# First context and leftover rows loaded behind the third group's queries, odd scores stored when made, value weights loaded later, orders pinned

## The chip, the cores and the metric

The kernel runs on one core of one Trainium2 chip. The metric is the device time of one execution in microseconds (us). Engines: PE (TensorE, with its weight load PEld), DVE (VectorE), ACT (ScalarE), POOL (GpSimd) and SP (SyncE, which here only issues DMAs). All data are fp32.

## The reference

A perceiver block: x (32 batches of 64 queries, 256 wide) gets a cross-attention over a context of 1601 keys of width 192, with 16 heads of 64, then an RWKV time mix and a feed-forward layer, each behind a layer norm and added to x.

```python
def xattn(query, context, w_q, w_kv, w_out, b_out):        # query = layernorm(x), 32 x 64 x 256; context 32 x 1601 x 192
    q = query @ w_q                                        # 16 heads x 64
    k, v = split(context @ w_kv)
    attn = softmax(einsum('bhqd,bhkd->bhqk', q, k) * 64**-0.5)
    return einsum('bhqk,bhkd->bhqd', attn, v) ... @ w_out + b_out
x = x + xattn(layernorm(x), ctx_768, w_q, w_kv, w_out, b_out)
x = x + rwkv(layernorm(x), ...)          # token shift, Wk/Wv/Wr, a scan over 512 steps, Wo
x = x + ffn(layernorm(x), w1, b1, w2, b2)
```

The change touches only the start of the cross-attention.

## The kernel before, in words

**Folding.** Keys and values are never made. The queries are multiplied by each head's key weights, so that a score is the product of a raw context row (192 wide) and a folded query (192 wide). The attention then averages raw context rows, and the value weights come after that.

**Query stage** (`queries`, L268, up to about 137 us). Four groups tg of 8 batches (512 tokens), each in two halves e of 8 heads. A half has 8 projections q_ps (L292), copied by ACT to a slot of `room[1]` (L299); the folds ql onto context columns 0 to 127 (L313), copied by DVE (L320) and ACT (L321) into q_lo, of which there are two buffers; the folds qh onto columns 128 to 191 (L341), copied by DVE (L348, L352; by ACT at L350 in the last half) into q_hi. Folded queries go to DRAM: two q_lo stores of 1 MB (L323) and two q_hi stores of 512 KB (L355) a half. The context has 1601 = 12 x 128 + 64 + 1 keys; the scores of the last, odd key are made apart (`odd_scores`, L242: matmuls L250, copies L257 and L258 into a buffer `od`) and stored by `odd_store` (four DMAs of 32 KB, L264). `turned_x` (L203) transposes the next group's normalised x; `normed_x` (L189) makes that on DVE. Where the order in the code leaves an engine free, the scheduler of the language places instructions by its own plan, unless `tc.issue_after(x)` pins an instruction behind x.

**Memory shared by stages.** Two large tiles, `room[0]` and `room[1]` (L381), hold weights and projected queries in the query stage. They have the tag of the two score buffers s_sb, so room[0] becomes s_sb of u = 0 and room[1] that of u = 1. `od` has the tag cT (L392), and so shares its two buffers with the transposed keys.

**Attention loop** (L972). u = 0 to 63 are halves of batches: b = u // 2, heads 8 j to 8 j + 7 with j = u % 2. `scores` (L649) makes six tiles of two key chunks, s_ps (L658, two PSUM buffers), each copied by ACT into s_sb (L665), with running maxima on DVE (L667 to L677). Behind the first tile of a batch the leftover 64 keys are scored (rest_ps, L635), from the rows of cT that a DMA copies (L374). `max_all` (L682) takes the maximum over partitions; `exps` subtracts it (DVE L703) and exponentiates (ACT L704), in three pieces, for u = 0 hung on tiles 3 to 5 of u = 1. The half before then gets its weighted sums: o_lo over context columns 0 to 127 (`av_lo`, L468 and, for leftover rows, L809, L819) and o_hi over the rest (`av_hi`, L864), with c_b, the raw context (`ctx_load`, L141), and rows_b, its 64 leftover rows (`rows_load`, L148). `total` (L763) and `inverse` (L776) make the denominators and `keep` (L792) stores them through ACT's queue.

**The order on SP.** Almost every DMA is issued by SP, in program order, each taking one of eight semaphores in turn, so that a ninth waits for the first. After the last query store (L355) SP issues rows_0 (L152), rest (L624), cb_1 (12 pieces of batch 1's keys in blocks, L170), q_1 (L180), c_0 (L143), the eight odd stores of the last group (`odd_late`, L413, run at L1051 to L1053 with `late_loads`), the value and output weights wv_lo, wv_hi, wo (L438 to L441), the RWKV weights (L448), biases and columns (L450 to L458), and then cT_1's row copy (L374).

Of the kernel before, what the change touches and what calls it, by code (L numbers as in the profile page):

```python
# [9 lines left out]
F32 = mybir.dt.float32  # L10
# [5 lines left out]
P = 128  # L16
# [4 lines left out]
def kernel(  # L21
# [38 lines left out]
    nc = tc.nc  # L60
# [6 lines left out]
    C2 = C - P  # L67
    NT = B * T // P
    NP = H // 2
# [5 lines left out]
    NS = C // C2  # L75
# [3 lines left out]
    KT = NBL * BL  # L79
    HALF = H // 2 * T  # L80
# [45 lines left out]
    with ExitStack() as st_b:  # L126
        with ExitStack() as st_a:
# [28 lines left out]
            def blocks_load(b):  # L156
# [16 lines left out]
                            )  # L173
                return c

            def q_load(b):

                q = kp.tile([P, NS, H * T], F32, tag="q", name=f"q_{b}")
                for r0 in (0, C2):
                    nc.sync.dma_start(  # L180
                        q[r0 : r0 + C2, :, :],
                        q_dram[b // QB][b % QB].rearrange("(s p) n -> p s n", p=C2),
                    )
                return q

# [82 lines left out]
            def queries(tg, xnT, copied, sp, sps, wq_sb, wkT, room, codn, kodT, wk_lo, wk_hi, od):  # L268
# [7 lines left out]
                for e in range(NP // 4):  # L276
# [5 lines left out]
                    for g in (2 * e, 2 * e + 1):  # L282
                        slot = (tg * NP // 2 + g) % 5
                        qT = room[1][:, slot * 2 * TG : (slot + 1) * 2 * TG].rearrange(
                            "p (k t) -> p k t", k=2
                        )
                        qTs.append(qT)
                        for k in range(2):
                            hp = 2 * g + k
                            pq = sps.tile([P, TG], F32, tag="ps", name=f"q_ps_{tg}_{hp}")  # L290
                            for c in range(2):
                                projected = nc.tensor.matmul(  # L292
                                    pq,
                                    lhsT=wq_sb[:, c, hp * P : (hp + 1) * P],
                                    rhs=xnT[:, c, :],
                                    start=(c == 0),
                                    stop=(c == 1),
                                )
                            nc.scalar.activation(qT[:, k, :], pq, AF.Copy, scale=HD**-0.5)  # L299
                    if e == 0 and tg == 0:  # L300
                        with tc.issue_after(projected.ins):
# [24 lines left out]
                        )  # L326
                    all_q.append(qTs)
                    for n in (0, 1) if e == 1 and tg == 0 else (e,) if tg else ():
                        odd_scores(tg, n, kodT, all_q[n], od[n], sps)
                        if more:  # L330
                            odd_store(tg, n, od[n])
                        else:
                            odd_late.append(lambda n=n: odd_store(tg, n, od[n]))
                    for k in range(2):
                        ph = [
                            sps.tile([P, QB, T], F32, tag="f", name=f"qh_ps_{tg}_{e}_{k}_{o}", bufs=6)
                            for o in range(2)
                        ]
                        for n in range(2):
                            for o in range(2):  # L340
                                nc.tensor.matmul(  # L341
                                    ph[o][n * C2 : (n + 1) * C2, :, :],
                                    lhsT=wkT[o * HD : (o + 1) * HD, 4 * e + 2 * n + k, P:C],
                                    rhs=qTs[n][o * HD : (o + 1) * HD, k, :],
                                    start=True,
                                    stop=True,
                                )
                        nc.vector.tensor_copy(hi[:, :, 2 * k, :], ph[0])  # L348
                        if e == 1 and not more:
                            nc.scalar.copy(hi[:, :, 2 * k + 1, :], ph[1])  # L350
                        else:
                            nc.vector.tensor_copy(hi[:, :, 2 * k + 1, :], ph[1])  # L352
                    for n in range(2):
                        ns = slice((8 * e + 4 * n) * T, (8 * e + 4 * n + 4) * T)
                        store = nc.sync.dma_start(  # L355
                            q_dram[tg][:, P:C, ns].rearrange("b p n -> p b n"),
                            hi[n * C2 : (n + 1) * C2].rearrange("p b h t -> p b (h t)"),
                        )
# [18 lines left out]
            with tc.tile_pool(name="setup", bufs=1) as sp, tc.tile_pool(  # L377
# [11 lines left out]
                ]  # L389
                wk_hi, codn = wk_hi[0:C2], codn[0:B]  # L390
                kodT = kodT.rearrange("p (h b) -> p h b", b=B)
                od = kp.tile([P, NS * KT], F32, tag="cT", name="od")  # L392
                od = [
                    od[:, k * 2 * TG : (k + 1) * 2 * TG].rearrange("p (o t) -> p o t", o=2)
                    for k in range(2)
                ]
                wq_sb = wq_sb.rearrange("p (c n) -> p c n", c=2)
                wkT = wkT.rearrange("p (h c) -> p h c", c=C)
                wqr = w_q.rearrange("(c p) n -> p c n", p=P)
# [10 lines left out]
                for n in range(4, NT, 4):  # L410
                    nc.sync.dma_start(x_sb[:, n : n + 4, :], xr[:, n : n + 4, :])
                b_tiles = {0: blocks_load(0)}
                odd_late = []  # L413
                for g in range(NP // 2):
                    ps = sps.tile([P, 2, C], F32, tag="ps", name=f"wkT_ps_{g}")
                    for k in range(2):
# [8 lines left out]
                for tg in range(B // QB):  # L425
                    turned, store = queries(tg, *turned, sp, sps, wq_sb, wkT, room, codn, kodT, wk_lo, wk_hi, od)
                    if tg == 1:
                        q_tiles = {0: q_load(0)}
                        cT = ctx_prep(0)

            nats = {}
            aw = st_a.enter_context(tc.tile_pool(name="late", bufs=1))
# [1 line left out]
            wv_hi = aw.tile([P, INNER], F32, name="wv_hi")  # L434
            wo_sb = aw.tile([P, INNER // P, D], F32, name="wo_sb")

            def late_loads():
                nc.sync.dma_start(wv_lo, w_kv[0:P, INNER : 2 * INNER])  # L438
                for r0 in (0, C2):
                    nc.sync.dma_start(wv_hi[r0 : r0 + C2, :], w_kv[P:C, INNER : 2 * INNER])  # L440
                nc.sync.dma_start(wo_sb, w_out.rearrange("(c p) n -> p c n", p=P))  # L441
                tags = iter(("xn", "in_k", "in_v", "in_r", "e", "ev", "num", "den"))
                for n, w in (("Wk", Wk), ("Wv", Wv), ("Wr", Wr), ("Wo", Wo)):
                    nats[n] = [
                        rp.tile([P, D], F32, tag=next(tags), name=f"nat_{n}_{c}") for c in range(2)
                    ]
                    for c in range(2):
                        nc.sync.dma_start(nats[n][c], w[c * P : (c + 1) * P, :])  # L448
                for n, v in enumerate((b_out, bo, b2)):
                    nc.sync.dma_start(bias_rows[:, n, :], v.partition_broadcast(P))  # L450
                with nc.allow_non_contiguous_dma(reason="per-channel vectors"):
                    for n, v in enumerate((time_decay, time_first)):
                        nc.sync.dma_start(cols[:, n, :], v.rearrange("(c p) -> p c", p=P))
                    for n, v in enumerate((mix_k, mix_v, mix_r)):
                        nc.sync.dma_start(
                            cols[:, 2 + n, :], v.rearrange("a b (c p) -> p (a b c)", p=P)
                        )
                    nc.sync.dma_start(b1_sb, b1.rearrange("(c p) -> p c", p=P))  # L458
# [223 lines left out]
            def max_all(u, mx):  # L682
                mb = ap.tile([P, HALF], F32, tag="mb", name=f"mb_{u}")
                nc.gpsimd.partition_all_reduce(mb, mx, P, bass_isa.ReduceOp.max)  # L684
                return mb
# [277 lines left out]
                        x_sb[:, i, :], x_sb[:, i, :], bias_rows[:, 0, :], ALU.add  # L963
                    )

            c_tiles = {}
            rests = [None, None]
            last = None
            before = None
# [2 lines left out]
            for u in range(2 * B):  # L972
# [2 lines left out]
                phase, i = (u - 5) % 4, (u - 5) // 4  # L975
                if before is not None:
                    before.out()
                if j == 0:
                    rows_load(b)
                out, mixer, older = outs[max(i, 0)], mixers[max(i, 0)], mixers[max(i - 1, 0)]  # L980
                fill = {}
# [18 lines left out]
                if u == 1:  # L1000

                    hooks = {3: parts[0:2], 4: parts[2:3], 5: parts[3:]}
                elif last is not None:
                    hooks = {
                        3: [last.inverse] + ([out.share] if phase == 1 and i >= 0 else []),
                        5: [last.keep],
                    }
                    last.total()
                else:
                    hooks = {}  # L1010
                s_sb, mx, top, done = scores(u, cT, q_tiles[b], hooks)
                if j == 0 and b + 1 < B:
                    with tc.issue_after(store.ins):
                        b_tiles[b + 1] = blocks_load(b + 1)
                        q_tiles[b + 1] = q_load(b + 1)
                mb = max_all(u, mx)
                if u == 1:
                    with tc.issue_after(top.ins):
# [8 lines left out]
                if u == 1:  # L1027
                    last.total()
                    last.inverse()
                    last.keep()  # L1030
                if j == 0 and 0 < b < B - 1:
                    cT_next = ctx_prep(b + 1)
                elif j == 1:
                    cT = cT_next
                if phase == 0 and i > 0:
# [6 lines left out]
                    mixer.norm()  # L1042
                if u == 2 * B - 2:
                    ready = stats_of(rp, list(range(4)), "ln3_0", "3")
                if j == 0:
                    c_tiles[b] = ctx_load(b)
                if phase == 3 and i >= -1:
                    odd_load(i + 1)
# [153 lines left out]
```

## Time and profile before

| | |
|---|---|
| time, median of 3 runs | 2555.59 us (2555.51 to 2556.14) |
| profiled execution | 2556.28 us, span 2554.5 us |
| PE busy | 2534.3 us (99%), 15618 instructions |
| DVE busy | 1925.0 us (75%) |
| ACT busy | 985.2 us (39%) |
| POOL busy | 411.2 us (16%) |
| first scores matmul of the attention loop | 137.14 us |
| first o_lo matmul of u = 0 with c_0 | 176.21 us |
| granted TensorE clock, mean | 0.999 |
| DMA | 174.23 MB, mean 68 GB/s |

Times in the profile are counted from the start of the span. A timeline row has start, us, engine, line, operation, out<-in, shapes and count, and in brackets the idle time of the engine ahead of it and what ended that. SPq is SP's sequencer, and its rows are the issuing of DMAs, not the transfers. A row of a table of waits names the instruction that waited and what released it.

### The profile page before, as it was taken

Reading aid. Unit: us, or ns where it says so; the run is one execution under the profiler, and the core shown is the slowest. Engines: PE = TensorE matmul, PEld = TensorE weight load, DVE = VectorE, ACT = ScalarE, POOL = GpSimd, SP = SyncE. Lnnn points to the kernel's source line nnn. Section 1 sums busy time; section 2 is a strip of 40 time slices with the busy share of each in tenths; the row PEclk is TensorE's granted clock in tenths of the full one; section 3 lists DMA queues with packets and bytes.
Section 4 is the critical chain, followed back from the end, with each engine's and each line's share of the span. In section 5 each row is a group of like instructions: output and inputs, shape, how many; then the busy total and the mean of one; then the engine's idle time right before and its main releaser. Section 6 shows DMA issues by size and latency. Waiting matters only on the chain.

```text
span 2554.5 us, 38114 instructions
## 1 busy us (share of the span) xinstructions
PE 2534.3 (99%) x15618; PEld 1215.2 (48%) x15618; DVE 1925.0 (75%) x2364; ACT 985.2 (39%) x1103; POOL 411.2 (16%) x372
## 2 busy tenths in 40 slices
PE   9989999999999999999999999999999999999999
PEld 3334444444444454444444454444444444444466
DVE  5477878878787878878787878878787878777731
ACT  3343434434333444333433344343433334344221
POOL 1002111121111121111111111111111111111100
PEclk9999999999999999999999999999999999999999
DMA  7786333333233223233332323233332322310100
GB/s 202 219 212 112 60 64 62 51 66 65 61 62 61 55 47 66 47 66 66 66 65 55 60 41 66 53 61 66 65 66 53 69 47 51 66 28 20 53 13 21
DMA packets 435967, 174.23 MB, mean 68 GB/s; under 512 B 334960, under 2 KB 421520, under 8 KB 435792
## 3 DMA queue, kind: packets, MB, share of 16 engines
q1 hardware_dynamic: 435408, 171.53, 32.7%
q8 instruction: 122, 2.00, 0.3%
q14 instruction: 53, 0.43, 0.1%
q10 hardware_dynamic: 384, 0.26, 0.0%
HBM read 141.07 MB, written 29.10 MB: 67 GB/s over the span
## 4 chain that ended last, share of the span: by engine, by line
PE 90%; DVE 4%; issue 2%; DMA 1%; SPq 1%; POOL 1%; ACT 1%; DVEq 0%; ACTq 0%; POOLq 0%
PE s_ps L658 35%; PE o_lo L468 24%; PE o_hi L864 11%; PE y_ps L468 2%; PE q_ps L292 2%; PE h_ps L1111 2%; PE fy L1127 2%; PE rest_ps L635 1%; PE o_hi L819 1%; PE v_ps L919 1%; PE ql_ps L313 1%; DVE s_sb L703 1%; PE o_lo L809 1%; DVE m L669 1%; PE v_ps L933 1%
## 5 line engine op out<-in xcount | busy, mean ns | idle before, releaser
L658 PE MATMUL s_ps<-q,cT 64*128 64x512 f32 x4608 | 1008.0, 590 | 2.3 <-ACT s_sb L665 1.4
L658 PEld LDWEIGHTS s_ps<-q,cT 64*128 64x128 f32 x4608 | 443.5, 187 | 516.5 <-issue 497.7
L468 PE MATMUL o_lo<-s_sb,c 128*64 128x512 f32 x3024 | 679.1, 596 | 5.8 <-DMA c<-in_ctx_dram 5.8
L665 ACT COPY s_sb<-s_ps 128x1024 f32<-128x1024 f32 x384 | 388.3, 1011 | 740.3 <-PE s_ps L658 732.2
L703 DVE TENSOR_TENSOR s_sb<-s_sb,mb 128x2048 f32<-128x2048 f32 x192 | 431.5, 2283 | 0.0
L704 ACT ACTIVATE s_sb<-s_sb 128x2048 f32<-128x2048 f32 x192 | 367.1, 1913 | 123.9 <-DVE s_sb L703 123.9
L468 PEld LDWEIGHTS o_lo<-s_sb,c 128*64 128x64 f32 x3024 | 209.3, 137 | 387.6 <-issue 383.3
L669 DVE TENSOR_TENSOR m<-m,s_sb 128x1024 f32<-128x1024 f32 x256 | 312.3, 1220 | 40.7 <-ACT s_sb L665 18.5
L864 PE MATMUL o_hi<-s_sb,c 128*64 128x256 f32 x3024 | 337.0, 379 | 0.0
L769 DVE TENSOR_TENSOR t<-t,s_sb 128x1024 f32<-128x1024 f32 x256 | 311.8, 1218 | 8.6 <-DVE t L769 0.5
L864 PEld LDWEIGHTS o_hi<-s_sb,c 128*64 128x64 f32 x3024 | 217.4, 137 | 135.9 <-issue 36.0
L772 POOL PARTITION_ALL_REDUCE den<-t x64 | 207.1, 3236 | 407.2 <-issue 381.6
L784 DVE STREAM_TRANSPOSE turned<-den 128x512 f32<-128x512 f32 x64 | 45.5, 711 | 275.6 <-POOL den L772 275.6
L693 ACT ACTIVATE rest<-rest 128x512 f32<-128x512 f32 x64 | 40.4, 631 | 405.5 <-DVE rest L692 363.5
L684 POOL PARTITION_ALL_REDUCE mb<-m x64 | 114.2, 1785 | 431.1 <-DVE m L677 417.3
L692 DVE TENSOR_TENSOR rest<-rest,mb 128x512 f32<-128x512 f32 x64 | 44.3, 692 | 108.0 <-POOL mb L684 107.9
L623 POOL MEMSET rest<- 64x256 f32 x128 | 39.2, 307 | 413.6 <-PE o_lo L809 307.7
L372 DVE STREAM_TRANSPOSE cT<-cb 128x768 f32<-128x768 f32 x96 | 89.5, 957 | 0.0
L667 DVE TENSOR_TENSOR m<-s_sb 128x1024 f32<-128x1024 f32 x64 | 77.6, 1212 | 9.1 <-ACT s_sb L665 9.1
L111 POOL TENSOR_TENSOR rstd_ln<-rstd_ln,root 128x1 f32<-128x1 f32 (+1 forms) x24 | 33.7, 1402 | 311.9 <-DVE rstd_ln L110 311.9
L809 PE MATMUL o_lo<-rest,rows 64*128 64x256 f32 x252 | 81.1, 402 | 0.0
L819 PE MATMUL o_hi<-rest,rows 64*128 64x256 f32 x252 | 81.1, 402 | 0.0
(164 smaller groups left out, 1829.3 us busy)
## 6 DMA issues: line engine op xcount, KB each, us to landing
q<-q_dram SPq DMA_DIRECT2D x64, 768.0 KB
c<-in_ctx_dram SPq DMA_DIRECT2D x32, 1152.0 KB
cb<-in_ctx_dram SPq DMA_DIRECT2D x192, 104.0 KB
cb<-in_ctx_dram SPq DMA_DIRECT2D x192, 96.0 KB
q_dram<-q_lo SPq DMA_DIRECT2D x16, 1024.0 KB
q_dram<-q_hi SPq DMA_DIRECT2D x16, 512.0 KB
rows<-in_ctx_dram SPq DMA_DIRECT2D x64, 32.0 KB
rest<-o_dram SPq DMA_DIRECT2D x128, 1.0 KB
```

Of the source, the lines that this page charges most:

```text
L468: last = nc.tensor.matmul(out[rs], lhsT=lhsT[:, rs], rhs=rhs, start=start, stop=stop, skip_group_check=True,)
L658: done = nc.tensor.matmul(ps[:, k, :], lhsT=cT[rs, s, i * P : (i + 1) * P], rhs=q[rs, s, js : js + HALF], start=(s == 0), stop=(s == NS - 1),)
L665: copied = nc.scalar.copy(s_sb[:, 2 * i : 2 * i + 2, :], ps)
L669: nc.vector.tensor_tensor(m2, m2, s_sb[:, 2 * i : 2 * i + 2, :], ALU.max)
L684: nc.gpsimd.partition_all_reduce(mb, mx, P, bass_isa.ReduceOp.max)
L703: nc.vector.tensor_tensor(s, s, m, ALU.subtract)
L704: nc.scalar.activation(s, s, AF.Exp)
L769: nc.vector.tensor_tensor(t2, t2, p[:, 2 * i : 2 * i + 2, :], ALU.add)
L772: nc.gpsimd.partition_all_reduce(self.den, t2[:, 0, :], P, bass_isa.ReduceOp.add)
L809: nc.tensor.matmul(self.po[:, k * HH : (k + 1) * HH], lhsT=self.rows[lo, 0, :], rhs=self.rest[lo, k * HH : (k + 1) * HH], start=(k == 0), ...
L819: nc.tensor.matmul(self.ph, lhsT=self.rows.rearrange("p n c -> p (n c)")[hi, c0 : c0 + P], rhs=self.rest[hi, (1 - k) * HH : (2 - k) * HH], ...
L864: nc.tensor.matmul(self.ph[o * C2 : (o + 1) * C2, :], lhsT=self.ctx[:, self.at[c], P:C], rhs=self.s_sb[:, c, o * HH : (o + 1) * HH], start ...
```

## The change

1. c_0 and rows_0 are loaded right behind the last store of the third group (tg = 2), ahead of the fourth group's stores; the loop no longer loads them for b = 0.
2. `od` leaves the tag cT. od[0] is now the tile m2 (tag m2, later the running maximum), and for the last group a slot of room[1]; od[1] is the part of room[1] behind the five query slots. In the last group the odd scores of n = 0 are stored when made; those of n = 1 stay where the late stores were.
3. wv_lo, wv_hi and wo are loaded in u = 2, behind the last of q_2's loads, and no longer in u = 0.
4. The projections q_ps of a half are pinned behind the last fold of the half before.
5. cT_0's preparation is pinned behind the last q_hi copy of group 1, cT_2's behind the last maximum of u = 2, and `keep` of u = 0 moves from u = 1 to the hook behind tile 2 of u = 2.

```diff
@@ q_load
-                    nc.sync.dma_start(
-                        q[r0 : r0 + C2, :, :],
-                        q_dram[b // QB][b % QB].rearrange("(s p) n -> p s n", p=C2),
+                    fetched.append(
+                        nc.sync.dma_start(
+                            q[r0 : r0 + C2, :, :],
+                            q_dram[b // QB][b % QB].rearrange("(s p) n -> p s n", p=C2),
+                        )
                     )
@@ queries
-                            for c in range(2):
-                                projected = nc.tensor.matmul(
+                            with tc.issue_after(folds[-1].ins) if folds else ExitStack():
+                                for c in range(2):
+                                    projected = nc.tensor.matmul(
...
                     for n in (0, 1) if e == 1 and tg == 0 else (e,) if tg else ():
+                        if not more and n == 0:
+
+                            at = (tg * NP // 2 - 1) % 5 * 2 * TG
+                            od[0] = room[1][:, at : at + 2 * TG].rearrange("p (o t) -> p o t", o=2)
                         odd_scores(tg, n, kodT, all_q[n], od[n], sps)
-                        if more:
+                        if more or n == 0:
                             odd_store(tg, n, od[n])
                         else:
                             odd_late.append(lambda n=n: odd_store(tg, n, od[n]))
...
-                                nc.tensor.matmul(
+                                fold = nc.tensor.matmul(
...
-                        nc.vector.tensor_copy(hi[:, :, 2 * k, :], ph[0])
+                        filed.append(nc.vector.tensor_copy(hi[:, :, 2 * k, :], ph[0]))
...
+                    folds.append(fold)
@@ setup
-                od = kp.tile([P, NS * KT], F32, tag="cT", name="od")
-                od = [
-                    od[:, k * 2 * TG : (k + 1) * 2 * TG].rearrange("p (o t) -> p o t", o=2)
-                    for k in range(2)
-                ]
+                m2 = ap.tile([P, 2, HALF], F32, tag="m2", name="od")
+                od = [m2, room[1][:, 10 * TG : 12 * TG].rearrange("p (o t) -> p o t", o=2)]
...
                     if tg == 1:
                         q_tiles = {0: q_load(0)}
-                        cT = ctx_prep(0)
+                        with tc.issue_after(filed[-1].ins):
+                            cT = ctx_prep(0)
+                    if tg == 2:
+                        with tc.issue_after(store.ins):
+                            rows_load(0)
+                            c_tiles = {0: ctx_load(0)}
@@ late loads
-            def late_loads():
+            def value_loads():
                 nc.sync.dma_start(wv_lo, w_kv[0:P, INNER : 2 * INNER])
...
                 nc.sync.dma_start(wo_sb, w_out.rearrange("(c p) n -> p c n", p=P))
+
+            def late_loads():
@@ attention loop
-                if j == 0:
+                if j == 0 and b:
                     rows_load(b)
...
+                    if u == 2:
+                        hooks[2] = [before.keep]
                     last.total()
...
                         q_tiles[b + 1] = q_load(b + 1)
+                        if u == 2:
+                            with tc.issue_after(fetched[-1].ins):
+                                value_loads()
...
                 if u == 1:
                     last.total()
                     last.inverse()
-                    last.keep()
                 if j == 0 and 0 < b < B - 1:
-                    cT_next = ctx_prep(b + 1)
+                    with tc.issue_after(top.ins) if b == 1 else ExitStack():
+                        cT_next = ctx_prep(b + 1)
...
-                if j == 0:
+                if j == 0 and b:
                     c_tiles[b] = ctx_load(b)
```

More of the change, by code (lines that the diff above doesn't have):

```diff
@@ L174, in blocks_load @@
                 return c
+            fetched = []
             def q_load(b):
@@ L290, in queries @@
                             pq = sps.tile([P, TG], F32, tag="ps", name=f"q_ps_{tg}_{hp}")
-                            for c in range(2):
-                                projected = nc.tensor.matmul(
[L293 to L298, printed above, removed]
+                            with tc.issue_after(folds[-1].ins) if folds else ExitStack():
+                                for c in range(2):
+                                    projected = nc.tensor.matmul(
+                                        pq,
+                                        lhsT=wq_sb[:, c, hp * P : (hp + 1) * P],
+                                        rhs=xnT[:, c, :],
+                                        start=(c == 0),
+                                        stop=(c == 1),
+                                    )
                             nc.scalar.activation(qT[:, k, :], pq, AF.Copy, scale=HD**-0.5)
@@ L412 @@
                 b_tiles = {0: blocks_load(0)}
-                odd_late = []
+                odd_late, filed, folds = [], [], []
                 for g in range(NP // 2):
@@ L964, in yproj @@
                     )
-            c_tiles = {}
             rests = [None, None]
```

## The prediction

> **What bounds the kernel now.** I read the page first: PE is busy 2534.3 of 2554.5 us, so some 20 us in the whole span are not matmul. The change touches the first 220 us only, and what it can win or lose there is the idle time of PE. The table of PE's waits (line, what it waited for, then us in total, times, longest) names that time:
>
> ```profile
> PE o_lo L468 <- DMA c<-in_ctx_dram: 5.8, 1, 5.8
> PE s_ps L658 <- ACT s_sb L665: 1.4, 4, 0.5
> PE ql_ps L313 <- ACT q_lo L321: 1.2, 1, 1.2
> PE rest_ps L635 <- DMA cT<-cT: 1.1, 1, 1.1
> PE ql_ps L313 <- DVE q_lo L320: 1.0, 1, 1.0
> PE s_ps L658 <- ACT q_hi L350: 0.8, 1, 0.8
> ```
>
> The largest is the first value product (o_lo) waiting for batch 0's context c_0. PE's timeline shows where the waits lie, and what follows them:
>
> ```profile
> 137.14 2.85 PE L658 MATMUL s_ps<-q,cT 64*128 64x512 f32 x12 [0.83 <-ACT q_hi L350]
> ...
> 176.21 12.52 PE L468 MATMUL o_lo<-s_sb,c 128*64 128x512 f32 x48 [5.81 <-DMA c<-in_ctx_dram]
> ...
> 194.37 2.74 PE L658 MATMUL s_ps<-q,cT 64*128 64x512 f32 x12
> 198.20 1.53 PE L635 MATMUL rest_ps<-q,cT 64*64 64x256 f32 x24 [1.08 <-DMA cT<-cT]
> 200.05 13.14 PE L658 MATMUL s_ps<-q,cT 64*128 64x512 f32 x60 [0.32 <-ACT s_sb L665]
> ```
>
> The 48 o_lo matmuls take 12.52 us here; in the next batches the chain of waits has them at 10.45. So the wait costs 5.81 + 2.07 us. The granted clock is 0.50 in 176 to 180 us and 0.99 after it. From the first scores tile to the second, it is 200.05 - 194.37 = 5.68 us at the third half against 141.38 - 137.14 = 4.24 at the first: 1.44 us for the waits on cT and s_sb.
>
> Why c_0 is late stands in SyncE's queue (issue time, us spent issuing, line) and in the stretches (us, then busy time of PE, PEld, DVE, ACT, POOL, granted clock, DMA share, GB/s):
>
> ```profile
> 132.56 4.59 SPq L323 DMA_DIRECT2D q_dram<-q_lo  x2
> 137.25 4.96 SPq L355 DMA_DIRECT2D q_dram<-q_hi  x2
> 142.31 7.16 SPq L152 DMA_DIRECT2D rows<-in_ctx_dram  x4
> 149.56 2.62 SPq L624 DMA_DIRECT2D rest<-o_dram  x4
> 152.24 8.43 SPq L170 DMA_DIRECT2D cb<-in_ctx_dram  x12
> 160.72 1.48 SPq L180 DMA_DIRECT2D q<-q_dram  x2
> 162.24 0.60 SPq L143 DMA_DIRECT2D c<-in_ctx_dram  x1
> 162.88 14.16 SPq L264 DMA_DIRECT2D o_dram<-od  x8
> ```
> ```profile
> 148.00:152.00 4.00, 4.00 (x22) 1.85 (x20) 2.34 (x2) 1.02 (x2) 0.00 (x0) 1.00 0.25 68
> 152.00:163.00 11.00, 11.00 (x54) 4.90 (x52) 7.29 (x7) 4.75 (x5) 1.80 (x1) 1.00 0.93 113
> 163.00:171.00 8.00, 7.40 (x38) 3.23 (x34) 7.79 (x6) 6.44 (x7) 0.20 (x1) 1.00 0.98 209
> ```
>
> Transfers run in the order of issue: the last query stores end at about 149 (a share of 0.25 in the 4 us from 148 is 1 us of work), then cb_1 (1.2 MB) to 162, q_1 (1.5 MB) to 170, c_0 behind them, landed at 176.1, and the eight odd stores after it.
>
> **Part by part.** S0 is the first scores matmul, 137.14.
>
> *1. c_0 and rows_0 issued before the last group's stores.* c_0 then lands before S0, and nothing else holds o_lo: its scores' last exponential ends at 173.63, but chunks are taken in an order that needs the first third (168.2) and second (170.9) first. **-5.81**, and **-2.07** for the clock. The price is 1.25 MB, some 5 us at the 252 GB/s of 171 to 176, put in front of the last six MB of stores.
>
> *2. Odd scores out of the key tile cT.* In the timeline cT_1 is transposed only at 178.52, after the odd stores (DMA 176.74 + 1.74 in the chain). Freed of them and of the weight loads on SyncE (177.15 to 194.57, ahead of cT_1's own DMA at 195.04), the rest keys land before they are needed. The odd store n = 0 of the last group is now issued when made; four such issues took 3.54 us of SyncE at 115.79, here between the two halves' stores, where SyncE has nothing else to issue: nothing. With keep of the first half moved behind the third score tile, ScalarE no longer stands in front of the copy that began at 198.98. **-1.44**.
>
> *3. The new wait.* One of the two odd buffers now lies in room[1], the memory that becomes s_sb_1. The late odd store (n = 1 of the last group, four DMAs) is still issued behind cb_1 and q_1. So ScalarE's first copy of the second half (157.14 before) waits until those stores have landed. Queued behind it on ScalarE are the other copies and the exponentials of half 0, hooked to copies 3 to 5; PE has two PSUM buffers, so it goes on for two tiles and stands at the third, which began at 157.14 + 2.36 = 159.50. When do they land? Call D the end of the query stores. From D to the end of q_1 it was 149 to 170 = 21 us, 3 of them idle (148 to 152) while rows and rest waited for free DMA slots; the rows are gone, so 18, and 1.5 to 2 to land (od: 1.74 after c_0's landing): D + 19 to 20, at most D + 23 if the idle time stays.
> D: before, the stores ran from 111.98 to 149, at shares of 0.84, 0.80, 0.78, 0.95, 1.00 and 0.96 in six stretches of 6 us: 4 us idle. After, group 2's last stores are issued about 7 us earlier (21 q_ps records, 9.3 us, ran ahead of its last ql; they are pinned behind it now; less the 2.8 of part 4, so 6.5). 149 - 6.5 + 5 - (0 to 4) is 143.5 to 147.5. It can't be before the last store is made and moved: S0' + 0.1, and 1 MB at 0.2 to 0.3 MB per us, 143.5 to 145. Both ends for D: 143.5, and 149 if nothing is won by the earlier start; I take 146, in the middle of them. Then the stores land at 165.0, the copy ends at 166.1, and PE, due at S0' + 22.4 = 162.3, stands **+3.8** us. From both sides: 1.3 to 10.8 (149 + 23 + 1.1 - 162.3).
>
> *4. q_ps pinned behind the previous half's folds.* The matmuls themselves stay; what goes is their use as filler. In half 1 of group 0, ten q_ps stood between 40.42 and 44.91 while VectorE normalised the next group; the first q_lo copy ends at 42.81 + 0.69:
>
> ```profile
> 42.81 1.88 DVE L320 COPY q_lo<-ql_ps 128x512 f32<-128x512 f32 x3
> ```
>
> so PE now stands from 40.42 to 43.5: +3.1. In group 1 the two q_ps at 70.94 (1.06 us of the way to the copies that end at 74.1) become waiting: +1.06. In the last group, where q_ps records ran between ql and its copies, each half is now whole, and the 1.22 on ACT q_lo goes, with a gap of 0.16 at 134.24: net **+2.8**. Bounds: +0.5 (the group 0 wait met by other work ready at 40.42, such as the transposes of the next group) and +4.2 (3.1 + 1.06 and nothing won). Thus S0' = 139.9.
>
> *5. Clock after the new stall.* At the measured 2.07 per 5.81 us of stall, 3.8 gives **+1.4** (0 to 2.1). The Trainium skill ("TensorE: Matmul & The Clock Gate", Part 1, What's actually happening) says that the gate falls to half after about one idle window of 3.4 us and rises again after one busy window; the 0.50 in 176 to 180 agrees. By it a stall under 3.4 us need cost nothing more and a longer one about 1.7 (an estimate from that page), so the sum would be 0.3 higher, and 1.1 lower for a stall of 3 us.
>
> *6. Weight loads later, orders pinned.* wv and wo are used first at 257.38 (the odd values), some 45 us after q_2's issue at 210.13; 2 MB need 8 us at 252 GB/s: hidden. cT_2 and keep in new places: at most one preparation (2.69 + 0.38 us on DVE) ends in front of PE, and at least nothing; I take **+1.0**.
>
> Sum: +2.8 + 3.8 + 1.4 + 1.0 - 5.81 - 2.07 - 1.44 = -0.3 on the profiled execution's 2556.28 us (span 2554.5 and 1.8 around it): 2556.0. The median of the runs is 2555.59, 0.7 lower; I forecast **2555.7**, nearly what the sum gives on the median, rounded up. The wait for c_0 is swapped for a wait for the odd stores, which stand behind the same two transfers.
>
> The Trainium skill ("DMA: Bandwidth & Descriptors", Queues, rings and completion order) has a rule that speaks against part 3: completion is not first in, first out per issuing engine, so a small store could overtake q_1 on engines that are done early. The trace shows c_0's landing at 176.1 and the first odd landing at 178.5, though issued 0.6 us apart. If the rule carried, the stores would land up to a microsecond or two sooner and the sum would be lower by that.
>
> **The rivals.**
> *A, the gain is realised.* The stores land while PE still has tiles to do or just after: D at its floor of 143.5, landing at 162.5, stall 0 to 1.3, no clock loss, nothing in front of PE in part 6, and a query stage between its lower bound and my value: +0.5 to 2.8, +0 to 1.3, -9.3: -8.8 to -5.2, central 2549. For it: shares of 0.78 to 0.84 before 130 show room to take in c_0 early. Against it: cb_1 and q_1 alone need 16 us at 113 and 209 GB/s, and PE is due 19 us after D's floor.
> *B, slower: the moved 1.25 MB pushes the whole queue.* From 130 to 148 the share is 0.95 to 1.00, so what goes in front there comes out at the end. D = 150.5 to 154, stores landing 170 to 174, or q_lo buffers (two) come free late and PE stands in the query stage instead; either way PE's third tile of half 1 starts at 171 to 175 instead of 159.5: +11.5 to 15.5 (the query stage's 2.8 is in it), +2.1 clock, +1.0, -9.3: +5.3 to +9.3, central 2563. It decides where D passes 149, that is, where the earlier start is worth less than the moved bytes.
> *C, c_0 still late*, so that the change doesn't do its first step: it would need c_0 to land past 170, 50 us after its issue; nothing in the queue is that long. I give it nothing.
>
> **How the numbers follow.** Forecast (stall swapped, own range 2551 to 2560.5): 0.50. A: 0.20. B: 0.30. A measurement tells about 0.2%, 5.1 us, from no change. A lies below 2550.5, B above 2560.7; so faster 0.20, same 0.50, slower 0.30. The range takes in A's centre and B's: 2548 to 2565.
>
> **What would show it.** Right: no wait on DMA c; a new row of s_ps waiting for ACT s_sb of 3 to 7 us at the second half's third tile, ScalarE's copy released by o_dram<-od; a q_lo wait on DVE near 43 of 3 us; S0' near 140; o_lo of half 0 at 10.45. Wrong: S0' over 142 (the stores hold the query stage), a copy released before 160 (A), or a stall over 9 us (B). An added wait at PE after 220 us that is not there before would mean that part 6 was priced too low.

## The result and the profile after

The changed kernel takes 2560.24 us (median of 22 runs, 2556.75 to 2563.45) against 2556.0 us for the kernel before (22 runs, 2555.31 to 2559.83): a ratio of 1.0015, 95% interval 1.0009 to 1.002. It is slower by 4.2 us, inside the 0.2% of no change, and inside the range; the upper end of the forecast's own range, 2560.5, is 0.3 us away. The forecast of 2555.7 missed by 4.5 us. Its terms can be checked one by one, because the profiled span grew by nearly as much as the median, by 4.0 us, from 2554.5 to 2558.5.

PE's waits in the changed kernel (line, what it waited for, us in total, times, longest):

```profile
PE s_ps L672 <- ACT s_sb L679: 8.2, 3, 7.3
PE wkT_ps L425 <- DMA room<-in_L_xattn_w_kv_dram: 4.4, 2, 4.1
PE ql_ps L318 <- DVE q_lo L325: 2.9, 1, 2.9
PE wkT_ps L426 <- DMA room<-in_L_xattn_w_kv_dram: 1.3, 2, 0.9
PE rw_ps_Wr L496 <- ACT Wk_T L501: 1.1, 1, 1.1
```

The wait for c_0 has gone, and so have those on cT and on ACT q_lo. In their place stand 7.3 us for ScalarE's copy of a score tile, 2.9 for q_lo in group 0 and 1.1 for the RWKV weights (`wkT_ps` waits for the first loads in both kernels). PE's timeline shows where:

```profile
44.06 1.97 PE L318 MATMUL ql_ps<-room,room 64*128 64x512 f32 x2 [2.92 <-DVE q_lo L325]
45.96 3.66 PE L254 MATMUL odd_ps<-room,room 64*32 64x512 f32 x32
49.55 2.65 PE L350 MATMUL qh_ps<-room,room 64*64 64x512 f32 x16
...
139.86 2.85 PE L672 MATMUL s_ps<-q,cT 64*128 64x512 f32 x12 [0.84 <-ACT q_hi L359]
...
169.70 12.64 PE L672 MATMUL s_ps<-q,cT 64*128 64x512 f32 x48 [7.31 <-ACT s_sb L679]
...
182.70 10.52 PE L482 MATMUL o_lo<-s_sb,c 128*64 128x512 f32 x48
```

The third tile of the second half starts at 169.70; o_lo of half 0 runs without a wait in 10.52. The chain of waits says what the third tile waited for (start, us, what):

```profile
141.16 9.21 DMA q_dram<-q_hi
150.39 0.52 SPq L170
...
156.56 7.41 DMA q<-q_dram
164.03 4.57 DMA nat_Wv<-in_L_attn_Wv_dram
168.63 1.02 ACT s_sb L679
169.70 12.64 PE s_ps L672 x48
```

In order stand the last query store, cb_1 (L170), q_1, then the copy. The chain names a load of an RWKV weight as the last releaser. The copy doesn't read it: SyncE's queue (issue time, us spent issuing, line) has the four late odd stores at 158.14, between q_1 and the RWKV weights, and the profile infers releasers from semaphores that the DMAs take in turn. By the semaphore events in the trace the four odd stores landed at 167.69 to 168.49, just ahead of the copy at 168.63, and the first load of nat_Wv only at 169.93:

```profile
116.95 5.50 SPq L152 DMA_DIRECT2D rows<-in_ctx_dram  x4
122.50 0.59 SPq L143 DMA_DIRECT2D c<-in_ctx_dram  x1
...
156.56 1.53 SPq L183 DMA_DIRECT2D q<-q_dram  x2
158.14 1.57 SPq L268 DMA_DIRECT2D o_dram<-room  x4
159.75 0.85 SPq L462 DMA_DIRECT2D nat_Wk<-in_L_attn_Wk_dram  x2
```

c_0 is issued 40 us earlier than before. Experiment e1 takes the odd stores away from there.

Laid beside each other, in us (the predicted column is the running sum of the prediction's terms):

| mark | before | after | difference | predicted |
|---|---|---|---|---|
| first scores matmul | 137.14 | 139.86 | +2.7 | +2.8 |
| third tile of half 1 | 159.50 | 169.70 | +10.2 | +6.6 |
| o_lo of half 0 | 176.21 | 182.70 | +6.5 | +2.2 |
| first tile of u = 2 | 194.37 | 198.87 | +4.5 | +0.1 |
| second tile of u = 2 | 200.05 | 202.99 | +2.9 | -1.3 |
| first tile of u = 3 | 232.67 | 236.75 | +4.1 | -0.3 |
| span | 2554.5 | 2558.5 | +4.0 | -0.3 |

Nearly the whole error, 3.6 of 4.3 us, is there at the second mark, the third tile of half 1.

### The profile page after: what moved, and what is told of

Read it like the earlier page. It is cut to its first block, busy times and chain, and to the rows that moved or that the text cites. A ratio compares the mean times of both kernels' runs of the same rounds, so it can differ in the third digit from the quotient of the medians.

```text
span 2558.5 us, 38118 instructions
## 1 busy us (share of the span) xinstructions
PE 2535.4 (99%) x15618; PEld 1214.2 (47%) x15618; DVE 1927.7 (75%) x2364; ACT 986.0 (39%) x1103; POOL 412.8 (16%) x372
## 4 chain that ended last, share of the span: by engine, by line
PE 93%; DVE 4%; DMA 1%; issue 1%; POOL 1%; ACT 0%; SPq 0%; DVEq 0%; ACTq 0%; POOLq 0%
PE s_ps L672 36%; PE o_lo L482 24%; PE o_hi L878 12%; PE y_ps L482 2%; PE q_ps L297 2%; PE h_ps L1129 2%; PE fy L1145 2%; PE rest_ps L649 2%; PE o_hi L833 1%; PE v_ps L933 1%; PE ql_ps L318 1%; DVE s_sb L717 1%; PE o_lo L823 1%; PE v_ps L947 1%; PE qh_ps L350 1%
## 5 line engine op out<-in xcount | busy, mean ns | idle before, releaser
L683 DVE TENSOR_TENSOR m<-m,s_sb 128x1024 f32<-128x1024 f32 x256 | 316.1, 1235 | 42.9 <-ACT s_sb L679 20.5
```

Of the source, the lines that this page charges most:

```text
L683: nc.vector.tensor_tensor(m2, m2, s_sb[:, 2 * i : 2 * i + 2, :], ALU.max)
```

## The experiments

Theory S is the prediction's: the new stall is the late odd store, which stands behind cb_1 and q_1. Rival Q is that the moved 1.25 MB push the whole queue; rival P that the pinned projections are the loss. Each run stood beside runs of the kernel before on the same chip (medians 2555.9 to 2556.5).

| run | what | us | ratio to before, 95% interval |
|---|---|---|---|
| e1 | after, all odd scores stored when made | 2552.29 | 0.9981 (0.9972 to 0.999) |
| e2 | after, no pins of q_ps | 2564.87 | 1.0035 (1.0021 to 1.0048) |
| e3 | before, c_0 and rows_0 early alone | 2564.32 | 1.0032 (1.002 to 1.0045) |
| e4 | before, new place of the odd scores alone | 2581.07 | 1.0098 (1.0084 to 1.0112) |
| e5 | e1, pins in groups 2 and 3 only | 2552.06 | 0.9984 (0.9975 to 0.9993) |
| e6 | e1, keep in its old place | 2558.79 | 1.001 (1.0001 to 1.0018) |
| e7 | e1, c_0 and rows_0 in their old place | 2560.77 | 1.0014 (1.0005 to 1.0023) |
| e8 | before, pins alone | 2559.82 | 1.0015 (1.0006 to 1.0024) |
| e9 | e1, pins in group 3 only | 2549.13 | 0.9971 (0.9959 to 0.9982) |
| e10 | e9, keep of u = 1 later | 2548.48 | 0.9969 (0.9957 to 0.9981) |
| e11 | e7, PE's order as in e1 | 2551.79 | 0.9982 (0.9973 to 0.9991) |
| e12 | e1, value weights in their old place | 2554.75 | 0.9991 (0.9982 to 1.0) |

**e1: the late odd store stored when made.**

```diff
-                        if more or n == 0:
-                            odd_store(tg, n, od[n])
-                        else:
-                            odd_late.append(lambda n=n: odd_store(tg, n, od[n]))
+                        odd_store(tg, n, od[n])
```

> The changed kernel, but the last group's odd scores of n = 1 are stored when made as well, ahead of the last q_hi stores, so that no store stands behind cb_1 and q_1. Theory S (the stall at the second half's third score tile is the wait for that late store, behind cb_1 and q_1): the first copy of the second half runs at 160, the 7.31 us stall and its slow clock (12.64 against 10.4 for 48 matmuls, 2.2) go: 2560.2 - 7.3 - 2.2 = 2550.7. Rival Q (the 1.25 MB moved ahead push the whole queue, so that something behind the query stores is late whatever is first): a wait of 4 to 7 us comes back at PE between 160 and 205, on cT, q or rest: 2556 to 2560. Rival P (the pinned q_ps are the loss): 2560 less the stall only as far as they allow, and first scores matmul still at 139.9; with S it is also there, so P is read from the next run.

2552.29, which is 8.0 less than the changed kernel. PE's timeline in u = 0 to 2:

```profile
142.23 28.59 PE L669 MATMUL s_ps<-q,cT 64*128 64x512 f32 x132
...
171.19 10.52 PE L479 MATMUL o_lo<-s_sb,c 128*64 128x512 f32 x48
...
193.37 13.14 PE L669 MATMUL s_ps<-q,cT 64*128 64x512 f32 x60 [1.81 <-ACT s_sb L676]
```

The eleven score tiles run in one piece, without the stall and at full clock. That shows the stall to be the wait for the late store. One small wait comes up later, 1.81 at u = 2's second tile: ScalarE's queue there has the exponentials of half 1, and these wait for DVE. Q's 4 to 7 us don't appear.

**e2: without the pins of q_ps.** `with tc.issue_after(folds[-1].ins) if folds else ExitStack():` becomes `with ExitStack():`.

> The changed kernel without the pins of q_ps behind the previous half's folds. Theory S: the first scores matmul comes back to about 137.1, but the third group's last stores are issued some 6 us later again, with the moved 1.25 MB behind them, so the query stores end at 149 to 154, the late odd store lands 19.3 later, and the second half's third tile starts at 170 to 174 (169.7 with pins): 2560 to 2565, nothing won. Rival P (the 2.7 us that the query stage is longer is the loss): 2557.4.

2564.87, 4.6 more than with pins; rival P falls. But the form was not the expected one: the first scores matmul came at 144.22, not at 137.1, because of a wait in the query stage, and the stall at the third tile was 6.44.

```profile
136.82 2.20 PE L318 MATMUL ql_ps<-room,room 64*128 64x512 f32 x4 [4.72 <-ACT q_lo L326]
...
144.22 2.85 PE L672 MATMUL s_ps<-q,cT 64*128 64x512 f32 x12 [0.85 <-ACT q_hi L359]
...
173.19 12.05 PE L672 MATMUL s_ps<-q,cT 64*128 64x512 f32 x48 [6.44 <-ACT s_sb L679]
```

```profile
136.21 1.29 DVE L325 COPY q_lo<-ql_ps 128x512 f32<-128x512 f32 x2 [5.29 <-DMA q_dram<-q_lo]
```

DVE's own wait at that place, 5.29 us, is on a q_lo store: both q_lo buffers stood behind c_0 in the queue. So the early load needs the pins, which bring group 2's last stores forward (107.86 against 111.81 here).

**e3: the early load alone.**

```diff
+                    if tg == 2:
+                        with tc.issue_after(store.ins):
+                            rows_load(0)
+                            c_tiles = {0: ctx_load(0)}
...
-                if j == 0:
+                if j == 0 and b:
                     rows_load(b)
...
-                if j == 0:
+                if j == 0 and b:
                     c_tiles[b] = ctx_load(b)
```

> The kernel before, with c_0 and rows_0 loaded behind the third group's last store and nothing else changed. Theory S: the wait for c_0 (5.81) and its slow clock (2.07) go, the wait on cT (1.4) stays, and the odd scores stay in the memory of cT, where nobody on PE waits for them before 178: 2556.0 - 7.9 = 2548.1. Rival Q: the moved bytes delay the last group's stores, PE stands for q_lo buffers or cT_1 waits longer for the odd stores (which land at 170 to 174 and hold DVE's transposes): 2552 to 2556.

2564.32: neither number. The waits are Q's, but they cost 8 to 12 us more than Q's 2552 to 2556. In the list of PE's waits:

```profile
PE ql_ps L313 <- ACT q_lo L321: 5.5, 2, 4.2
PE s_ps L662 <- ACT s_sb L669: 5.0, 3, 4.7
...
PE rest_ps L639 <- DMA cT<-cT: 3.4, 1, 3.4
```

The wait for c_0 has gone, yet nothing is won. 4.2 us go to the q_lo buffers, as in e2. And at u = 2 the waits on cT (1.1 before, 3.4 now) and on s_sb (4.7, ScalarE itself standing 8.10 us for the denominators rden) take what the c_0 wait had covered.

**e4: the new place of the odd scores alone**, which adds their wait to the old order.

> The kernel before, with the new place of the odd scores alone: m2 and room[1], n = 0 of the last group stored when made, n = 1 late, behind cb_1, q_1 and here c_0 too. Theory S: the first copy of the second half waits until that store lands at about 177, the third tile starts at about 178.5 instead of 159.5 (+19), the wait for c_0 disappears inside it (-7.9) and the cT wait (-1.4), the clock loss comes back (+2.2): 2556 + 12 = 2568. Against it (the copy waits for something else than the store): 2554 to 2556.

2581.07. ScalarE's copy and PE's third tile:

```profile
177.75 1.93 ACT L666 COPY s_sb<-s_ps 128x1024 f32<-128x1024 f32 x2 [21.96 <-DMA o_dram<-room]
...
194.03 1.01 ACT L666 COPY s_sb<-s_ps 128x1024 f32<-128x1024 f32 x1 [4.61 <-DMA b_sb<-in_L_ffn_b_dram]
```
```profile
178.81 12.37 PE L659 MATMUL s_ps<-q,cT 64*128 64x512 f32 x48 [18.93 <-ACT s_sb L666]
...
222.72 15.17 PE L659 MATMUL s_ps<-q,cT 64*128 64x512 f32 x60 [8.89 <-ACT s_sb L666]
```

Here the profile names the odd store as the releaser. The stall was expected at 19 and is 18.93. Of the 13 us above the forecast, 10.6 stand at PE in two waits that I had not priced: 1.71 on the exponentials, behind 4.61 at ScalarE, whose own two stores of the leftover exponentials take their semaphores in turn with SyncE's small loads and came behind them (they were issued at 192.70 and 193.79, when the loads that had held these two semaphores landed, at 192.62 and 193.76); and 8.89 at u = 2, where ScalarE stood 8.09 for rden.

**e6: keep of u = 0 in its old place**, which tells what that wait for rden is.

```diff
-                    if u == 2:
-                        hooks[2] = [before.keep]
...
                     last.inverse()
+                    last.keep()
```

> The kernel of e1 with keep of u = 0 back in its old place, in u = 1, ahead of the copies of u = 2 on ScalarE. Theory K (the c_0 wait had covered a second limit, the inverse denominators of u = 0 at 199.5, for which ScalarE stands with keep at the head of its queue): the first copy of u = 2 goes from 192.3 to about 199.7 and PE's second tile of u = 2 from 193.4 to 200.9: 2552.3 + 7 = 2559. If keep's place is worth only the 0.3 us that PE showed for it before: 2552.5.

2558.79, 6.5 more than e1. ScalarE:

```profile
201.13 1.01 ACT L676 COPY s_sb<-s_ps 128x1024 f32<-128x1024 f32 x1 [8.09 <-DVE rden L799]
```

PE stands 9.37 us at u = 2's second tile. Theory K holds: behind the wait for c_0 lay a second limit, rden, for which ScalarE stood 8.09 us with keep at its head, the same 8.09 as in the kernel before.

**e8: the pins alone**, on the kernel before.

> The kernel before with the pins of q_ps alone. The query stage gets 2.7 longer, its last stores come forward, c_0 lands at 171 to 173, so the c_0 wait goes to 0 to 1. By theory K (keep of u = 0 and the denominators at 61.5 us after the first scores matmul hold u = 2's second tile, at 202.8 against 200.05): 2556 + 2.7 = 2559, with a wait of 4 to 7 us on ACT s_sb in place of the c_0 wait. If the c_0 wait was a loss by itself: 2556 + 2.7 - 7.9 = 2551.

2559.82. Waits of PE in order:

```profile
139.98 2.85 PE L660 MATMUL s_ps<-q,cT 64*128 64x512 f32 x12 [0.84 <-ACT q_hi L351]
...
174.23 10.52 PE L470 MATMUL o_lo<-s_sb,c 128*64 128x512 f32 x48 [0.99 <-DMA c<-in_ctx_dram]
...
197.44 2.60 PE L637 MATMUL rest_ps<-q,cT 64*64 64x256 f32 x24 [4.31 <-DMA cT<-cT]
...
202.90 15.65 PE L660 MATMUL s_ps<-q,cT 64*128 64x512 f32 x60 [2.85 <-ACT s_sb L667]
```

The pins alone cut the wait for c_0 from 5.81 to 0.99, and nothing comes of it: 4.31 on cT and 2.85 on s_sb replace it, and u = 2's second tile starts at 202.90, against an expected 202.8.

**e7 and e11: the load in its old place, the rest as in e1.**

> The kernel of e1 with c_0 and rows_0 loaded in their old place, behind q_1. If the early load is worth the 7.9 us of the old wait: 2560. If the pinned order by itself brings the stores, and so c_0, forward: without 1.25 MB ahead of them the query stores end at 145 to 146, c_0 lands 27 later at 172 to 173, o_lo is due at 171.2: a wait of 1 to 2 us, partly behind the 1.8 us at u = 2's second tile: 2552 to 2554.

2560.77, but for a reason that was not asked: the scheduler now put u = 2's first score tile ahead of o_lo, and PE stood 9.21 us for it, so e7 says nothing on the load:

```profile
182.36 5.40 PE L665 MATMUL s_ps<-q,cT 64*128 64x512 f32 x12 [9.21 <-issue]
187.69 10.52 PE L475 MATMUL o_lo<-s_sb,c 128*64 128x512 f32 x48
```

e11 pins that tile behind the last o_hi of u = 0:

```diff
+                            with tc.issue_after(halves_done[0].high.ins) if u == 2 and i == 0 else ExitStack():
```

> The kernel of e7 (c_0 and rows_0 in their old place) with the first score tile of u = 2 pinned behind the last o_hi of u = 0, so that PE keeps the order of e1; in e7 the plan put that tile, which waits for cT_1, ahead of o_lo. Now o_lo waits for c_0 alone: landing at about 36 us after the first scores matmul, o_lo due 33.2 after it, a wait of 2 to 3.5, of which up to 1.8 lies behind the wait at u = 2's second tile: 2552.3 + 0.5 to 3 = 2553 to 2555. If the early load is worth the old 7.9: 2560.

2551.79, the time of e1 (2552.29) and not 8 us more:

```profile
173.58 12.22 PE L475 MATMUL o_lo<-s_sb,c 128*64 128x512 f32 x48 [2.25 <-DMA c<-in_ctx_dram]
```

With pins, keep and odd scores changed, c_0 from its old place is 2.25 us late, and o_lo is 1.70 slower behind that wait. But two waits of e1 are gone here, 1.81 for the exponentials at u = 2's second tile and 1.49 for ACT Wk_T. From the first scores matmul to the first tile of u = 3 the two profiles take 90.12 us (e11) and 89.55 (e1). The early load, the change's first item, wins next to nothing by itself.

**e5, e9: which pins pay.** `if folds` becomes `if tg > 1` (e5) and `if tg > 2` (e9).

> The kernel of e1 (all odd scores stored when made) with the q_ps pins only in groups 2 and 3, so that q_ps can fill PE's waits in groups 0 and 1 again. If the pins cost what the 2.92 and 0.88 us waits show and help only through the stores of groups 2 and 3: 2552.3 - 3 = 2549.3, first scores matmul 2.5 to 3 us earlier. If the early pins help the stores too: a wait for q_lo stores or a later first scores tile, 2552 to 2556.

2552.06, as e1: the 2.92 us wait went from group 0 to group 1, whose filler, group 2's projections, was still pinned.

> The kernel of e1 with the q_ps pins in the last group alone, so that q_ps of groups 1 and 2 can fill PE's waits in the halves before them (in e5 the 2.92 us wait only moved from group 0 to group 1, whose filler is group 2's q_ps, pinned there). If the pins pay only by bringing group 2's last stores ahead of group 3's projections: the 2.92 goes, about 1 us stays, 2552.2 - 3 = 2549. If the pins of the earlier groups pay too, through earlier stores: a q_lo wait or a later copy, 2552 to 2556.

2549.13, 3.2 less than e1, as expected: only group 3's pins pay. What leaving out the earlier pins saves is not the wait of 2.92 us itself. e12 (below) has that wait, with the clock at 1.00 behind it in its profile, and starts its scores no later than e9 without the wait; e1, with the slow clock, starts them at 138.00:

```profile
135.52 2.85 PE L669 MATMUL s_ps<-q,cT 64*128 64x512 f32 x12 [0.84 <-ACT q_hi L356]
...
135.43 2.85 PE L669 MATMUL s_ps<-q,cT 64*128 64x512 f32 x12 [0.84 <-ACT q_hi L356]
```

The first row is e9's, the second e12's.

**e10: keep of u = 1 later**, `hooks.pop(5)` in u = 2 and `hooks[2] = [before.keep]` in u = 3.

> The kernel of e9 with keep of u = 1 moved from u = 2 (tile 5) to u = 3 (tile 2), so that ScalarE no longer stands at it ahead of the copies of the transposed RWKV weights. If the 1.5 us that rw_ps_Wr waited for ACT Wk_T is lost time: 1.5 below e9, 2547.5. If DVE is the next limit there: the wait comes back at s_ps on ACT s_sb, and the time is that of e9.

2548.48 (2548.11 to 2549.38) against 2547.82 to 2549.48 for e9: not told apart. The wait for ACT Wk_T doesn't stand in e9's profile either, so the run doesn't price it; 1.96 us on ACT s_sb stand at u = 3's sixth tile, behind the keep that was moved there. e9 and e10 are the fastest kernels here, 0.3% under the kernel before.

**e12: the value weights in their old place.**

> The kernel of e1 with the value and output weights loaded in their old place, in u = 0, ahead of the RWKV weights. If their place is hidden, as it was costed: 2552.3. If the 2 MB (8 us of the queue) push cT_1's row copy and the stores of the leftover exponentials, which take their semaphores in turn with SP's DMAs: rest_ps waits on cT and ScalarE on a DMA around 185 to 195, 2 to 4 us in all, 2554 to 2556.

2554.75, 2.5 more than e1, with the 95% intervals overlapping. Its profile has a wait on cT at u = 2, because the row copy came behind the weight loads on SyncE (issued at 188.71, against 182.52 in e1):

```profile
191.02 1.91 PE L646 MATMUL rest_ps<-q,cT 64*64 64x256 f32 x24 [3.49 <-DMA cT<-cT]
```

From the first scores matmul to the first tile of u = 3 it takes 91.32 us, 1.8 more than e1's 89.55. The later load is worth about that, once nothing else is late there; in part 6 it was costed at nothing.

## Why the prediction came out as it did

**Right.** The swap and its outcome: the wait for c_0 gives way to a wait for the odd stores (e1, e4), and the net is within 0.2%. Terms that held: the c_0 wait and its slow clock gone (-1.99 between o_lo and u = 2's first tile beside the -5.81; priced 2.07), cT and s_sb (-1.6; priced -1.44), the small waits (+1.1; priced +1.0, by luck, since it is a wait of 1.07 for ACT Wk_T behind keep of u = 1, which part 6 had not named), and 2.2 for the clock after the stall (48 score matmuls in 12.64 against 10.4 at the pace of e1's 132 in 28.59), where 1.4 was priced.

The rule behind that 1.4, a price in proportion to the stall, does not hold. The clock stands at 0.50 for 6.8 us each time: from 173.4 to 180.3 in the kernel before, from 44.2 to 51.0 and from 167.1 to 173.9 in the changed one. What it costs is half of the part that falls on work: 2.07 behind the wait of 5.81, 2.2 behind 7.31, but 3.3 behind 2.92, where all of it did.

**The term that was mis-sized** is the stall in part 3: +3.8 was taken, 7.31 was measured, inside its bounds of 1.3 to 10.8 and just over the 3 to 7 given as its sign. The sum D + 19 held: query stores ended at 149 (the DMA share is 0.98 in 142 to 148 and 0.50 in 148 to 150), the last odd store landed at 168.49, and SyncE's next load on the odd stores' semaphores, nat_Wr, went out at 168.20. What failed was D = 146. The end of the query stores did not move: the last one landed at 149.86 before and at 150.38 after. That is the case "nothing is won by the earlier start", the upper end of D and the border to rival B. I had group 2's last q_lo stores coming 6.5 us earlier; they were issued at 107.86 against 111.98, 4.1 earlier, and the 5 us of moved bytes used that up. The reason for the missing 2.4 is a cost in group 0 that I had left out:

```profile
38.00:44.00 6.00, 3.13 (x15) 1.19 (x12) 4.50 (x16) 1.75 (x3) 1.01 (x1) 1.00 0.00 1
44.00:48.00 4.00, 3.94 (x26) 1.06 (x34) 1.79 (x4) 0.58 (x1) 0.00 (x0) 0.52 0.60 208
48.00:52.00 4.00, 4.00 (x32) 0.69 (x16) 1.98 (x3) 1.17 (x2) 0.00 (x0) 0.62 0.99 323
```

In these stretches of the changed kernel (the third number from the end is the granted clock) the wait of 2.92 us is followed by a clock of 0.52 and 0.62. The profile of e12 has the same wait without the slow clock, which gives the price:

```profile
42.90 1.12 PE L318 MATMUL ql_ps<-room,room 64*128 64x512 f32 x2 [2.92 <-DVE q_lo L325]
43.95 1.95 PE L254 MATMUL odd_ps<-room,room 64*32 64x512 f32 x32
45.83 1.95 PE L347 MATMUL qh_ps<-room,room 64*64 64x512 f32 x16
```

(1.97 - 1.12) + (3.66 - 1.95) + (2.65 - 1.95) = 3.3 us, behind a wait of 2.9. The moved loads took more of the queue as well: SyncE spent 5.50 us issuing rows_0, and the DMA share was 0.39 in 122 to 125.

**Right by cancelling.** The query stage's +2.8 came to +2.7, but not by my terms. To group 1's second half it grew by 6.7 (2.92 + 3.3 for the clock, and 0.5 that was there before the wait), and from there to the first scores matmul it shrank by 4.0 (74.13 us against 78.11), where I had priced -0.3.

**Right in the sum, wrong in the attribution.** I put -7.88 on the early load and -1.44 on keep and cT together. e3, e6, e8 and e11 show that these were not separate gains: with the load alone moved nothing is won, with keep alone back 6.5 are lost, and with the load alone back nothing is lost. The gain needs three things at once: c_0 earlier (by the load or by the pins), keep out of ScalarE's way, and cT_1's row copy no longer behind the loads on SyncE. Lines in the old trace said so. The copy at u = 2 began at 198.98, behind keep, which had waited for rden, ready at 198.65. That did not move with c_0: keep is issued 61.6 us behind the first scores matmul in the kernel before and, with c_0 early, in e3 and e6.

**Two readings that were wrong.** Part 2 took the odd stores for what held cT_1. In the old trace DVE was busy with the half's last maximum until 178.60, and the transposes at 178.52 followed it without idle time; they were done at 181.62, and what came late was the row copy, issued at 195.04 behind the weight loads. How much the new place of the odd scores adds there no run shows alone. And the paragraph on completion order took 178.5 for the first odd landing. By the semaphore events that is one of the last store, issued at 176.74; the first, issued 0.6 us behind c_0, had landed at 175.49, ahead of c_0's last piece at 176.07. So a small store does overtake a large load here, by 0.6 us, less than the microsecond or two allowed for it.

**Rivals.** B's mechanism is real, but only without pins: e2 and e3 have its q_lo wait and its time (2564.87 and 2564.32 for a priced 2563). A needed the stores out of the queue's back, not a faster queue; e9 gives its time (2549.13 for a priced 2549), and e1 comes near it. C did not occur: c_0 landed at 129.17.

**The spread from run to run.** Most kernels with the 2.92 us wait spread over 4 to 6.7 us (the changed one 6.7, e1 6.3), e9 and e10 without it over 1.7 and 1.3. The mean granted clock is on record for every run, and one slow stretch of 6.8 us lowers it by 0.0013. In e1 the two runs at 1.000 took 2547.31 and 2547.76 us, the eight at 0.998 or 0.999 took 2550.87 to 2553.66. In e12 the three at 0.999 took 2549.32 to 2551.32, the seven at 0.997 took 2554.68 to 2555.79. So much of the spread in these two goes with the clock, and e12's profile shows one of its fast runs. Behind which wait the clock fell in a run without a profile is not on record, and the clock is not all: e5, with every run at 0.999, spreads over 2.6, and the kernel before, without the wait, over 4.5.

The Trainium skill ("TensorE: Matmul & The Clock Gate", Part 1, What's actually happening) puts the gate's step at about one idle window of 3.4 us. The profiles here have it step down after 2.92 us in seven of eight cases, and after waits of 2.19 (e9) and 2.25 (e11) us, while 2.19 us in e5 and in e10 left it at 1.00. So a wait below the page's figure does not keep the clock; the measured rows decide.

## What to carry to other kernels

When a buffer is moved into memory that another stage takes over, the last reader of that buffer becomes a wait of the next stage: look up where that reader, here four stores of 32 KB, stands in its queue, and add up what stands in front of it. Before a wait is priced as a gain, look for what would have released the same engine a moment later (here a copy that began 0.3 us after its denominators): a gain is at most the distance to that. And a pin that costs filler early can pay through stores later; pin only where the queue needs it (group 3 here), since a PE wait that is made up elsewhere can still leave a slow clock behind it.

## What the runs showed of the hardware

In these profiles the granted clock stands at 1.00 or at 0.50, and a slow stretch behind a wait lasts 3.4 us or a multiple of it: 6.8 in the kernel before and behind seven of the eight waits of 2.92 us, 3.4 in e9, 10.2 in e6, e7 and e8, 20.5 in e4. So a wait of 2.92 us cost 3.3 us more than itself in the changed kernel, a wait of 5.81 cost 2.07 more before, and 2.92 cost nothing more in e12. Waits of 2.2 us were followed by a slow stretch in some kernels and not in others (60 score matmuls took 14.76 us in e9 and 13.15 in e10), and so was a wait of 1.05 us in e3 (0.52 in 76 to 78 us), while one of 1.04 in the kernel before was not.

A store on ScalarE's queue stood 4.6 us behind small loads that SyncE had issued (e4), though no data joined them: the two queues take their completion semaphores from one rotation in this program (in the kernel before, two stores of ScalarE at 166.44 and 166.95 take the two semaphores between those of SyncE's first and second late odd store).
